# A graph layer's last stage: squares moved behind the next pair's scaling, layer norm in groups of six

## The chip, the cores and the metric

The kernel runs on one core of a Trainium2 chip. The metric is the device time of one execution in microseconds (us); several executions are timed and their median is given. A profile of one execution shows each engine: TensorE (PE, with its weight loads PEld), VectorE (DVE), ScalarE (ACT), GpSimd (POOL) and SyncE (SP), whose queue issues most of the DMAs here.

## The reference

A graph convolution with a mixture of experts, batch norm over the nodes, a residual and a layer norm. There are 6250 nodes of 256 features, 200000 edges and 64 experts, two per node. Cut to what matters:

```python
x = gc + (feats @ W_res + b_res)            # graph convolution and residual weights
core = _moe_ff(x, Wg, bg, w1, b1, w2, b2)   # per node: g1 * expert_1(x) + g2 * expert_2(x)
y = x + core
mean = jnp.mean(y, axis=0)                  # batch norm over the 6250 nodes
var = jnp.mean((y - mean) ** 2, axis=0)
bn = (y - mean) * rsqrt(var + 1e-5) * gamma + beta
z = feats + bn
out = (z - z.mean(-1)) / sqrt(z.var(-1) + 1e-5)   # layer norm over the 256 features
```

## The kernel before

Most of the program (degrees, gathering of neighbours, routing, the 64 experts) is the same before and after. What follows the experts is one block, from line 1552 on, and its instructions keep the order in which the code writes them, engine by engine.

The nodes stand as 50 tiles of 125 nodes (`NT = 50`, `TP = 125`) by 256 features (`D`). `x_all` (or `x`) holds x of all tiles in SBUF, `fb` the features plus beta, also of all tiles. The experts have written their outputs to `y_dram`, two rows per node.

**The gates' stage** takes the tiles in 25 pairs. For each pair it loads `yr` (both experts' rows, 512 KB, eight buffers in the pool `gat`). ACT multiplies the second expert's rows by their gate (line 1576, one instruction for each tile), DVE multiplies the first's by theirs and adds them to x (1578), and DVE adds the second's (1580). ACT squares the pair into `sq` (1582, four buffers of two tiles). TensorE multiplies x and `sq` by a matrix of ones and accumulates the sums over all nodes in `pm` (1584) and `pv` (1586). Two f32 matmuls of 256 columns go to each for every pair.

Then DVE and ACT make `mean`, `scale` (gamma over the standard deviation) and `less` (mean times scale), each 125 x 256 with the same values in all rows (1588 to 1598).

**The layer norm** goes over groups of tiles: 1, 2, 3, then eight groups of five, then 3 and 1. For each group, `scaled` multiplies x by scale on DVE (1622). `sums` adds the features, less offset, to a tile and takes the sum of each node over its features (`accum_out`, 1631); one small instruction turns the sums into minus means `lm` (1633). `squares` on ACT squares with the bias `lm` and sums (1640), one root per group (1642). `rows_out`, one group later, makes the reciprocal `ssq` (1647) and the product of `lm` with it (1648), writes the normalised rows to `o` (DVE 1652 for two tiles of five, ACT 1654 for the rest), and sends them out in two DMAs (112 and 13 partitions).

The features less offset come in two ways. For groups of five, TensorE forms them in PSUM (`pf`, two buffers, 1617): `fb` has a spare partition 125, in which one DMA puts the row `less` for 40 tiles (1610), and the matrix `unit` is an identity with a last row of -1, so that one matmul gives fb - less. `shifted` issues the five matmuls of a group two groups ahead. For the smaller groups DVE subtracts `less` from `fb` in place (1625).

Of the kernel before, what the change touches and what calls it, by code (L numbers as in the profile page):

```python
# [9 lines left out]
F32 = mybir.dt.float32  # L10
# [5 lines left out]
AF = mybir.ActivationFunctionType  # L16
ALU = mybir.AluOpType
# [14 lines left out]
D = 256  # L32
# [117 lines left out]
def gnn_moe_kernel(ctx, tc, x_in, x_cols, src, dst, bases, nexts, firsts, parts, lasts, W_gc, b_gc, W_res, b_res, Wg, bg, w1, b1, w2, b2,  # L150
                   gamma, beta, out):
    nc = tc.nc
    V, S, G, T = nc.vector, nc.scalar, nc.gpsimd, nc.tensor
# [66 lines left out]
    for a in range(0, NS * WMAX, 128):  # L220
        b = min(a + 128, NS * WMAX)
        V.tensor_scalar(iota_h[:, a:b, :], iota_f[:, :b - a, None].to_broadcast([128, b - a, 2]), float(a), None,
                        op0=ALU.add)
# [16 lines left out]
    with tc.tile_pool(name="edges", bufs=1) as ep, ExitStack() as later:  # L240
# [18 lines left out]
        for c, (g0, k, w, n) in enumerate(DENSE):  # L259
            a = g0  # L260
            while a < g0 + k * n:
                b = min(a - a % 2 + LANES // w // 2 * 2, g0 + k * n)
# [3 lines left out]
                a = b  # L266
# [20 lines left out]
        with tc.tile_pool(name="late", bufs=1) as lp, tc.tile_pool(name="both", bufs=2) as bp, \  # L287
# [24 lines left out]
            part = dp.tile([128, 2, ND], F32, name="part")  # L312
# [12 lines left out]
            for k, w in enumerate((W_gc, W_res)):  # L325
                nc.sync.dma_start(out=wcat[:, :, k * D:(k + 1) * D],
                                  in_=w.rearrange("(k p) d -> p k d", p=128))
# [4 lines left out]
            a, wides = 0, []  # L332
            for c, (g0, k, w, n) in enumerate(DENSE):
                if c == ND - 1 or DENSE[c + 1][2] != w:
# [3 lines left out]
                    a = c + 1  # L338
# [11 lines left out]
            for k, values in enumerate((LOW, HIGH)):  # L350
                c = 0
                while c < NC:
                    m = 1
# [139 lines left out]
            for i in range(NGR // CG):  # L493
# [32 lines left out]
                for c in range(CG):  # L526
# [66 lines left out]
        with tc.tile_pool(name="xs", bufs=1) as xs, tc.tile_pool(name="hotg", bufs=2) as hg, \  # L593
# [73 lines left out]
            groups = [(c, j, i) for c, (g0, k, w, n) in enumerate(DENSE) for j in range(n) for i in range(k)]  # L667
# [94 lines left out]
            made = {"below": 0, "above": NT, "gathered": len(GATHER)}  # L762
# [192 lines left out]
            now, n = 0.0, 0  # L955
# [18 lines left out]
            with tc.For_i(0, n_groups, 1) as gi:  # L974
# [6 lines left out]
                                op1=ALU.mult)  # L981
# [3 lines left out]
                                       op0=ALU.mult, op1=ALU.add)  # L985
# [18 lines left out]
                start = ge.tile([128, 1], F32, name="start")  # L1004
# [39 lines left out]
    x = x_all[:TP]  # L1044
# [59 lines left out]
    with tc.tile_pool(name="xw", bufs=1) as xw, tc.tile_pool(name="xl", bufs=3) as xl, \  # L1104
# [42 lines left out]
        with tc.manual_schedule():  # L1147
            sums = {}
            for t0 in range(ta, tb, 2):
                n = min(2, tb - t0)  # L1150
# [8 lines left out]
            for t0, z in sums.items():  # L1159
                n = min(2, tb - t0)  # L1160
# [392 lines left out]
    with tc.tile_pool(name="fin", bufs=1) as fp, tc.tile_pool(name="gat", bufs=8) as gp, \  # L1553
            tc.tile_pool(name="fl", bufs=2) as fl, \
            tc.tile_pool(name="ps_f", bufs=2, space=PSUM) as ps_f, \
            tc.tile_pool(name="ps_m", bufs=1, space=PSUM) as ps_m, tc.manual_schedule():
        unit = fp.tile([128, TP], F32, name="unit")
        below = fp.tile([128, 1], F32, name="below")
        V.tensor_scalar(below, pidx, float(TP), -1.0, op0=ALU.is_ge, op1=ALU.mult)
        V.tensor_scalar(unit, ident[:, :TP], below, None, op0=ALU.add)  # L1560
        eps = fp.tile([TP, 2], F32, name="eps")
        V.memset(eps, LN_EPS)

        S.activation(eps[:, 1:2], eps[:, 0:1], AF.Sqrt)
        pm = ps_m.tile([TP, D], F32, name="pm")
        pv = ps_m.tile([TP, D], F32, name="pv")
        for t0 in range(0, NT, 2):
            yr = gp.tile([128, 2, 2, D], F32, name="yr")
            for t in range(t0, t0 + 2) if t0 < 4 else (t0,):
                n = 1 if t0 < 4 else 2  # L1570
                loads.clear()
                node_in(yr[:, t - t0:t - t0 + n].rearrange("p t j d -> p t (j d)"), y_rows, t, n)
                for u in written[-AHEAD:-1] if t == 0 else ():
                    tc.add_manual_dep(loads[0].ins, u.name, SYNCED, reason="the last writes")
            for t in range(t0, t0 + 2):
                S.activation(yr[:TP, t - t0, 1, :], yr[:TP, t - t0, 1, :], AF.Copy, scale=gates[:, 1, t:t + 1])  # L1576
            for t in range(t0, t0 + 2):
                V.scalar_tensor_tensor(x[:, t, :], yr[:TP, t - t0, 0, :], gates[:, 0, t:t + 1], x[:, t, :],
                                       op0=ALU.mult, op1=ALU.add)
            V.tensor_tensor(x[:, t0:t0 + 2, :], x[:, t0:t0 + 2, :], yr[:TP, :, 1, :], ALU.add)  # L1580
            sq = fl.tile([TP, 2, D], F32, name="sq", bufs=4)
            S.activation(sq, x[:, t0:t0 + 2, :], AF.Square)  # L1582
            for t in range(t0, t0 + 2):
                T.matmul(pm, ones[:TP, :TP], x[:, t, :], start=(t == 0), stop=(t == NT - 1))
            for t in range(t0, t0 + 2):
                T.matmul(pv, ones[:TP, :TP], sq[:, t - t0, :], start=(t == 0), stop=(t == NT - 1))
        mean = fp.tile([TP, D], F32, name="mean")
        V.tensor_scalar(mean, pm, 1.0 / N, None, op0=ALU.mult)
        msq = fp.tile([TP, D], F32, name="msq")
        V.tensor_mul(msq, mean, mean)  # L1590
        scale = fp.tile([TP, D], F32, name="scale")
        V.scalar_tensor_tensor(scale, pv, 1.0 / N, msq, op0=ALU.mult, op1=ALU.subtract)
        V.tensor_scalar(scale, scale, 0.0, BN_EPS, op0=ALU.max, op1=ALU.add)
        S.activation(scale, scale, AF.Sqrt)
        V.reciprocal(scale, scale)  # L1595
        V.tensor_mul(scale, scale, gam)
        less = fp.tile([TP, D], F32, name="less")
        V.tensor_mul(less, mean, scale)


        part = {}
        groups, t0 = [], 0
        for n in [1, 2, 3] + [5] * ((NT - 10) // 5) + [3, 1]:
            groups.append((t0, n))
            t0 += n
        assert t0 == NT

        five = [g for g in groups if g[1] == 5]
        f0, f1 = five[0][0], sum(five[-1])
        nc.sync.dma_start(out=fb[TP:TP + 1, f0:f1, :], in_=less[0:1, None, :].to_broadcast([1, f1 - f0, D]))  # L1610

        def shifted(t0, n):
            if n < 5:
                return
            pf = ps_f.tile([TP, 5, D], F32, name="pf", padded_shape=[TP, 6, D])
            for u in range(5):
                T.matmul(pf[:, u, :], unit[:TP + 1, :], fb[:TP + 1, t0 + u, :], start=True, stop=True)
            part["pf", t0] = pf

        def scaled(t0, n):  # L1620
            xs = x[:, t0:t0 + n, :]
            V.tensor_tensor(xs, xs, scale[:, None, :].to_broadcast([TP, n, D]), ALU.mult)  # L1622
            if n < 5:
                fs = fb[:TP, t0:t0 + n, :]
                V.tensor_tensor(fs, fs, less[:, None, :].to_broadcast([TP, n, D]), ALU.subtract)  # L1625

        def sums(t0, n):
            lm = fl.tile([TP, 5], F32, name="lm", bufs=3)
            for t in range(n):
                f = part["pf", t0][:, t, :] if n == 5 else fb[:TP, t0 + t, :]  # L1630
                V.scalar_tensor_tensor(x[:, t0 + t, :], x[:, t0 + t, :], 1.0, f, op0=ALU.mult,  # L1631
                                       op1=ALU.add, accum_out=lm[:, t:t + 1])
            V.tensor_scalar(lm[:, :n], lm[:, :n], -1.0 / D, None, op0=ALU.mult)  # L1633
            part[t0] = lm

        def squares(t0, n):
            ssq = fl.tile([TP, 5], F32, name="ssq", bufs=3)
            for t in range(n):
                sq = fl.tile([TP, D], F32, name="sq2")
                S.activation(sq, x[:, t0 + t, :], AF.Square, bias=part[t0][:, t:t + 1],  # L1640
                             accum_out=ssq[:, t:t + 1])
            S.activation(ssq[:, :n], ssq[:, :n], AF.Sqrt, scale=1.0 / D, bias=eps[:, 0:1])
            part["ssq", t0] = ssq

        def rows_out(t0, n):
            rs, lm = part.pop(("ssq", t0)), part.pop(t0)
            V.reciprocal(rs[:, :n], rs[:, :n])
            V.tensor_mul(lm[:, :n], lm[:, :n], rs[:, :n])
            o = fl.tile([TP, 5, D], F32, name="o")
            m = 2 if n == 5 else 0  # L1650
            for t in range(m):
                V.tensor_scalar(o[:, t, :], x[:, t0 + t, :], rs[:, t:t + 1], lm[:, t:t + 1], op0=ALU.mult, op1=ALU.add)  # L1652
            for t in range(m, n):
                S.activation(o[:, t, :], x[:, t0 + t, :], AF.Identity, scale=rs[:, t:t + 1], bias=lm[:, t:t + 1])  # L1654
            node_dma(nc.sync, False, o[:, :n, :], node_rows(out, t0, n))

        ahead_of = {i: g for i, g in zip(range(2, len(groups)), five)}
        for i, g in enumerate(groups):
            if i in ahead_of:
                shifted(*ahead_of[i])  # L1660
            scaled(*g)
            sums(*g)
            squares(*g)
            if i:
                rows_out(*groups[i - 1])
        rows_out(*groups[-1])


# [54 lines left out]
```

## Time and profile before

| what | us |
|---|---|
| median of 3 runs | 1546.34 (1545.77 to 1549.16) |
| the profiled execution, its own time | 1543.25 |
| span of its profile | 1541.5 |
| busy: PE 90%, DVE 68%, POOL 51%, ACT 48% of the span | 1380.2, 1047.4, 784.1, 745.3 |
| first load of y issued | 1418.0 after the span's start |
| `less` finished | 1483.5 |
| last ACT instruction ends | 1538.0 |

The span runs from the first to the last instruction; the profiled execution's own time is 1.75 us longer. Times in the views are us from the start of the span. The busy shares are means over stages that have different limits; the part that the change edits is the last 124 us, so its own rows are what to read.

### The profile page before, as it was taken

What the parts mean: (1) busy time and instruction counts of PE and PEld (TensorE: products, weight loads), DVE (VectorE), ACT (ScalarE), POOL (GpSimd) and SP (SyncE); (2) the same over time, 40 slices, a digit from 0 to 9 for tenths busy, and PEclk for the clock granted to TensorE, in tenths of its full rate; (3) what the DMA queues carried; (4) which work ended last, traced back from release to release, by engine and by line L of the source; (5) the groups of instructions that cost most, each with busy time, mean ns of one, the idle gap of its engine ahead of it and who ended that gap; (6) DMA issues with size and microseconds to landing.
All of it is one profiled execution on the core that took longest, in us unless ns stands there. A gap on an engine that the chain in (4) does not pass through costs nothing. (4 is left out here: it accounts for less than half of the span.)

```text
span 1541.5 us, 33071 instructions
## 1 busy us (share of the span) xinstructions
PE 1380.2 (90%) x9987; PEld 1147.4 (74%) x9987; DVE 1047.4 (68%) x2943; ACT 745.3 (48%) x1891; POOL 784.1 (51%) x878
## 2 busy tenths in 40 slices
PE   5999478899999999999999967799999999997963
PEld 3555267788888899999999956688888877875642
DVE  9999889989888888888777749333223233222687
ACT  4675544456666566665555524322222222222668
POOL 7000226777776677766666620376566665652000
PEclk9999699999999999999999978899999999998986
DMA  6899665777777787777777737478687887874804
GB/s 192 263 287 327 241 212 162 209 226 224 210 220 221 204 235 214 217 214 219 218 204 216 203 94 245 130 255 268 203 277 253 277 272 219 250 243 152 286 22 147
DMA packets 209177, 336.41 MB, mean 218 GB/s; under 512 B 22283, under 2 KB 140758, under 8 KB 208989
## 3 DMA queue, kind: packets, MB, share of 16 engines
q1 hardware_dynamic: 154201, 180.36, 37.2%
q0 software_dynamic: 47888, 146.77, 32.4%
q10 hardware_dynamic: 6900, 7.07, 1.6%
q8 instruction: 81, 1.33, 0.4%
q14 instruction: 107, 0.88, 0.2%
HBM read 254.55 MB, written 73.10 MB: 213 GB/s over the span
## 5 line engine op out<-in xcount | busy, mean ns | idle before, releaser
L613 POOL DMA_INDIRECT r<-h_dram,srcg x445 | 468.9, 1054 | 244.1 <-PE pc L699 79.4
L745 PE MATMUL sm<-hrow,counts 128*128 128x258 f32 x1470 | 486.9, 346 | 8.4 <-DVE counts L736 8.3
L719 ACT CAST counts<-pc 128x196 f32 (+7 forms) x879 | 356.9, 406 | 209.0 <-PE pc L699 175.0
L746 PE MATMUL sm<-hrow,counts 128*128 128x256 f32 x1470 | 394.6, 282 | 0.0
L699 PE MATMUL pc<-hotk,lo 128*128 128x245 bf16 (+7 forms) x1118 | 305.0, 304 | 41.7 <-DVE counts L736 19.9
L745 PEld LDWEIGHTS sm<-hrow,counts 128*128 128x128 f32 x1470 | 286.6, 195 | 26.4 <-issue 11.9
L686 DVE TENSOR_TENSOR hotk<-key,iota_h 128x784 bf16<-128x784 f16 (+4 forms) x488 | 246.8, 506 | 58.1 <-PE pc L699 56.0
L746 PEld LDWEIGHTS sm<-hrow,counts 128*128 128x128 f32 x1470 | 279.8, 190 | 1.3
L1442 ACT ACTIVATE hT<-ph,b1c 128x112 f32<-128x112 f32 (+16 forms) x256 | 109.9, 430 | 325.4 <-PE ph L1440 309.9
L736 DVE TENSOR_TENSOR counts<-pc,counts 128x49 f32 x908 | 217.6, 240 | 48.8 <-ACT counts L719 12.3
L1452 PE MATMUL py<-w2s,hT 128*128 128x256 f32 (+7 forms) x992 | 238.0, 383 | 0.0
L1440 PE MATMUL ph<-xgT,w1s 128*128 128x112 f32 (+17 forms) x1024 | 203.0, 342 | 0.6 <-DVE xgT L1430 0.6
L1452 PEld LDWEIGHTS py<-w2s,hT 128*128 128x128 f32 (+7 forms) x992 | 161.0, 170 | 42.2 <-DVE ys L1455 2.5
L1440 PEld LDWEIGHTS ph<-xgT,w1s 128*128 128x128 f32 x1024 | 167.7, 192 | 31.1 <-issue 11.2
L1405 POOL DMA_INDIRECT y_dram<-ys,dest x124 | 119.1, 960 | 112.2 <-DVE ys L1455 63.7
L1455 DVE TENSOR_TENSOR ys<-py,b2s 128x256 f32<-128x256 f32 (+7 forms) x124 | 52.3, 422 | 176.9 <-PE py L1452 167.5
L1405 POOL DMA_INDIRECT xg<-x_dram,ids x124 | 120.3, 970 | 91.9 <-DVE ids L1362 52.9
L699 PEld LDWEIGHTS <-lo 128*128 128x128 bf16 x1118 | 99.5, 100 | 74.7 <-issue 17.4
L618 PE MATMUL pg<-r,hot 128*128 128x258 f32 x445 | 144.6, 325 | 3.1 <-DMA r<-h_dram,srcg 2.3
L1430 DVE TENSOR_SCALAR xgT<-pte,bsum 128x112 f32<-128x112 f32 (+14 forms) x128 | 48.8, 423 | 125.9 <-PE pte L1427 125.8
L619 PE MATMUL pg<-r,hot 128*128 128x256 f32 x445 | 125.1, 281 | 0.0
L457 PE MATMUL pr<-wcat,f 128*128 128x512 f32 x196 | 99.6, 632 | 3.2 <-DMA wcat<-in_L_gnn_W_res_dram 3.2
(330 smaller groups left out, 1724.7 us busy)
## 6 DMA issues: line engine op xcount, KB each, us to landing
w1s<-in_L_gnn_w_dram SPq DMA_DIRECT2D x64, 512.0 KB
w2s<-in_L_gnn_w_dram SPq DMA_DIRECT2D x64, 512.0 KB
y_dram<-zeros SPq DMA_DIRECT2D x48, 256.0 KB
yr<-y_dram SPq DMA_DIRECT2D x22, 512.0 KB
b2s<-in_L_gnn_b_dram SPq DMA_DIRECT2D x64, 128.0 KB
h_dram<-hrow SPq DMA_DIRECT2D x5, 1536.0 KB
r<-h_dram,srcg POOLq DMA_INDIRECT x445
f<-in_x_cols_dram SPq DMA_DIRECT2D x25, 256.0 KB
```

The lines of the kernel that those rows point to most:

```text
L613: G.indirect_dma_start(out=f32(r[:, :2 * D]), out_offset=None, in_=h_dram[:, :], in_offset=bass.IndirectOffsetOnAxis(ap=idx, axis=0))
L618: T.matmul(pg, hot, r[:, D:], start=first, stop=False)
L619: T.matmul(pg[:, :D], hot, r[:, :D], start=False, stop=last)
L686: V.tensor_tensor(hot, pairs(key, e, n, m), iota_h[:, None, :m, :].to_broadcast([128, n // 2, m, 2]), ALU.is_equal)
L699: T.matmul(pc, los[g // PAIRS][:, r // 2, :, r % 2], hots.pop(g), start=(i == 0), stop=(i == k - 1))
L719: put = S.copy(counts[c % 2][:, :, 1:][:, :, ds(at, w - 1)], pc[:, :, 1:])
L736: add = V.tensor_tensor(to, more, f32(had), ALU.add).ins
L745: T.matmul(sm, by, hrow[:, t, D:], start=(t == 0), stop=False)
L746: T.matmul(sm[:, :D], by, hrow[:, t, :D], start=False, stop=(t == NS - 1))
L1405: w = G.indirect_dma_start(**kw)
L1440: T.matmul(ph[:, :m], w1s[:, kk, c * 128:(c + 1) * 128], xgT[:, kk, :m], start=(kk == 0), stop=(kk == 1))
L1452: T.matmul(py[:n], hT[:, c, k * 128:k * 128 + n], w2s[:, c, :], start=(c == 0), stop=(c == 3))
```

## The change

In the gates' stage, the squares and sums of a pair (`summed`) are issued behind the next pair's loading, scaling and adding (`joined`), and `sq` has three buffers instead of four. On ACT, before (`yr_...` and `sq_...` are buffers, one number for each pair):

```order
L1576 ACTIVATE yr_21525<-yr_21525,gates_16387 125x256 x2
L1582 ACTIVATE sq_21532<-x_all_16381 125x512
L1576 ACTIVATE yr_21538<-yr_21538,gates_16387 125x256 x2
L1582 ACTIVATE sq_21545<-x_all_16381 125x512
L1576 ACTIVATE yr_21551<-yr_21551,gates_16387 125x256 x2
```

And from the start of the stage in the changed kernel:

```order
L1584 ACTIVATE yr_21477<-yr_21477,gates_16387 125x256 x2
L1584 ACTIVATE yr_21485<-yr_21485,gates_16387 125x256 x2
L1593 ACTIVATE sq_21493<-x_all_16381 125x512
L1584 ACTIVATE yr_21499<-yr_21499,gates_16387 125x256 x2
L1593 ACTIVATE sq_21506<-x_all_16381 125x512
```

The first square (of the first pair) now stands behind the scaling of the second pair, and so on to the end, where two squares follow each other.

TensorE forms the features less offset for all tiles, two tiles to a matmul (512 columns). The first six tiles are written from `fb` before the gates' stage and left open; when `less` is known, three matmuls of a row of -1 (`minus`, one partition) with `less` close them. The rest comes as before from `fb` with its row of less, now for 44 tiles. On TensorE, the end of the program before, from the last `pv` on:

```order
L1584 MATMUL pm_21469<-x_all_16381,ones_16372 125x256 x2
L1586 MATMUL pv_21470<-sq_21794,ones_16372 125x256 x2
L1617 MATMUL pf_21840<-fb_17227,unit_21462 125x256 x5
L1617 MATMUL pf_21868<-fb_17227,unit_21462 125x256 x5
L1617 MATMUL pf_21902<-fb_17227,unit_21462 125x256 x5
```

The same place in the changed kernel:

```order
L1595 MATMUL pm_21475<-x_all_16381,ones_16372 125x256 x2
L1597 MATMUL pv_21476<-sq_21800,ones_16372 125x256 x2
L1620 MATMUL pf_21471<-less_21816,minus_21469 125x512 x3
L1634 MATMUL pf_21823<-fb_17227,unit_21462 125x512 x3
L1634 MATMUL pf_21870<-fb_17227,unit_21462 125x512 x3
```

The three matmuls with `minus` are new there; `pf_21471` was opened ahead of the first `pm`.

In the layer norm the groups are 1, 2, 3, six groups of six, 4, 3, 1. A group's `scaled` stands one group ahead of its `sums`; the subtraction of less from fb on DVE is gone; `lm` keeps sums, and the factor of minus one over 256 goes into the square's scale and into the product with the reciprocal. Of groups of up to four, the rows go into buffers of the pool `gat` instead of `o`. DVE writes two rows of each group from the fourth on (one of the last, which is one tile). On DVE, behind `less`, before:

```order
L1598 TENSOR_TENSOR less_21810<-mean_21800,scale_21804 125x256
L1622 TENSOR_TENSOR x_all_16381<-x_all_16381,scale_21804 125x256
L1625 TENSOR_TENSOR fb_17227<-fb_17227,less_21810 125x256
L1631 SCALAR_TENSOR_TENSOR x_all_16381,lm_21815<-x_all_16381,fb_17227 125x256
L1633 TENSOR_SCALAR lm_21815<-lm_21815 125x1
L1622 TENSOR_TENSOR x_all_16381<-x_all_16381,scale_21804 125x512
L1625 TENSOR_TENSOR fb_17227<-fb_17227,less_21810 125x512
L1631 SCALAR_TENSOR_TENSOR x_all_16381,lm_21824<-x_all_16381,fb_17227 125x256 x2
L1633 TENSOR_SCALAR lm_21824<-lm_21824 125x2
L1647 RECIPROCAL ssq_21818<-ssq_21818 125x1
L1648 TENSOR_TENSOR lm_21815<-lm_21815,ssq_21818 125x1
```

And in the changed kernel:

```order
L1615 TENSOR_TENSOR less_21816<-mean_21806,scale_21810 125x256
L1638 TENSOR_TENSOR x_all_16381<-x_all_16381,scale_21810 125x256
L1638 TENSOR_TENSOR x_all_16381<-x_all_16381,scale_21810 125x512
L1644 SCALAR_TENSOR_TENSOR x_all_16381,lm_21828<-x_all_16381,pf_21471 125x256
L1638 TENSOR_TENSOR x_all_16381<-x_all_16381,scale_21810 125x768
L1644 SCALAR_TENSOR_TENSOR x_all_16381,lm_21835<-x_all_16381,pf_21471 125x256 x2
L1659 RECIPROCAL ssq_21830<-ssq_21830 125x1
L1660 SCALAR_TENSOR_TENSOR lm_21828<-lm_21828,ssq_21830 125x1
L1638 TENSOR_TENSOR x_all_16381<-x_all_16381,scale_21810 125x1536
L1644 SCALAR_TENSOR_TENSOR x_all_16381,lm_21851<-x_all_16381,pf_21471 125x256 x3
```

Scaling of the next group stands ahead of a group's sums, and the first sum reads `pf` in PSUM where it read `fb`. The diff, cut:

```diff
+SIZES_OUT = [1, 2, 3] + [6] * 6 + [4, 3, 1]
+PIECES = list(range(0, 43, 6)) + [46, N // TP]
...
+        minus = fp.tile([1, TP], F32, name="minus")
+        V.memset(minus, -1.0)
+        pf = [ps_f.tile([TP, 6, D], F32, name="pf")]
+        for t in range(0, 6, 2):
+            T.matmul(pf[0][:, t:t + 2, :], unit[:TP, :], fb[:TP, t:t + 2, :], start=True, stop=False)
...
-            sq = fl.tile([TP, 2, D], F32, name="sq", bufs=4)
+
+        def summed(t0):
+            sq = fl.tile([TP, 2, D], F32, name="sq", bufs=3)
             S.activation(sq, x[:, t0:t0 + 2, :], AF.Square)
...
+        for t0 in range(0, NT, 2):
+            joined(t0)
+            if t0:
+                summed(t0 - 2)
+        summed(NT - 2)
...
+        nc.sync.dma_start(out=fb[TP:TP + 1, 6:, :], in_=less[0:1, None, :].to_broadcast([1, NT - 6, D]))
+        for u in range(0, 6, 2):
+            T.matmul(pf[0][:, u:u + 2, :], minus, less[0:1, None, :].to_broadcast([1, 2, D]), start=False, stop=True)
...
+        def shifted(k):
+            pf.append(ps_f.tile([TP, 6, D], F32, name="pf"))
+            a, b = PIECES[k:k + 2]
+            for t in range(a, b, 2):
+                T.matmul(pf[k][:, t - a:t - a + 2, :], unit[:TP + 1, :], fb[:TP + 1, t:t + 2, :], start=True, stop=True)
...
-            if n < 5:
-                fs = fb[:TP, t0:t0 + n, :]
-                V.tensor_tensor(fs, fs, less[:, None, :].to_broadcast([TP, n, D]), ALU.subtract)
...
-            V.tensor_scalar(lm[:, :n], lm[:, :n], -1.0 / D, None, op0=ALU.mult)
...
-                S.activation(sq, x[:, t0 + t, :], AF.Square, bias=part[t0][:, t:t + 1],
+                S.activation(sq, x[:, t0 + t, :], AF.Square, scale=-float(D), bias=part[t0][:, t:t + 1],
...
-            V.tensor_mul(lm[:, :n], lm[:, :n], rs[:, :n])
-            o = fl.tile([TP, 5, D], F32, name="o")
-            m = 2 if n == 5 else 0
+            V.scalar_tensor_tensor(lm[:, :n], lm[:, :n], -1.0 / D, rs[:, :n], op0=ALU.mult, op1=ALU.mult)
+            if n > 4:
+                o = fl.tile([TP, 6, D], F32, name="o")
+            else:
+                o = gp.tile([128, 2, 2, D], F32, name="yr").rearrange("p t j d -> p (t j) d")[:TP]
+            m = 0 if t0 < 6 else min(n, 2)
...
+        scaled(*groups[0])
+        made = 1
         for i, (t0, n) in enumerate(groups):
+            if made < len(PIECES) - 1 and (i > 2 or made < 2):
+                shifted(made)
+                made += 1
+            if i + 1 < len(groups):
+                scaled(*groups[i + 1])
+            sums(t0, n)
+            squares(t0, n)
             if i:
                 rows_out(*groups[i - 1])
```

More of the change, by code (lines that the diff above doesn't have):

```diff
@@ L1564, in gnn_moe_kernel, with joined @@
         S.activation(eps[:, 1:2], eps[:, 0:1], AF.Sqrt)
+        minus = fp.tile([1, TP], F32, name="minus")
[3 more added lines that the diff above has]
+            T.matmul(pf[0][:, t:t + 2, :], unit[:TP, :], fb[:TP, t:t + 2, :], start=True, stop=False)
         pm = ps_m.tile([TP, D], F32, name="pm")
         pv = ps_m.tile([TP, D], F32, name="pv")
-        for t0 in range(0, NT, 2):
+        def joined(t0):
             yr = gp.tile([128, 2, 2, D], F32, name="yr")
@@ L1598, in gnn_moe_kernel @@
         V.tensor_mul(less, mean, scale)
+        nc.sync.dma_start(out=fb[TP:TP + 1, 6:, :], in_=less[0:1, None, :].to_broadcast([1, NT - 6, D]))
+        for u in range(0, 6, 2):
+            T.matmul(pf[0][:, u:u + 2, :], minus, less[0:1, None, :].to_broadcast([1, 2, D]), start=False, stop=True)
         part = {}
         groups, t0 = [], 0
-        for n in [1, 2, 3] + [5] * ((NT - 10) // 5) + [3, 1]:
+        for n in SIZES_OUT:
             groups.append((t0, n))
@@ L1606, in gnn_moe_kernel @@
         assert t0 == NT
[L1608 to L1612, printed above, removed]
-            if n < 5:
[L1614 to L1618, printed above, removed]
+        def shifted(k):
[3 more added lines that the diff above has]
+                T.matmul(pf[k][:, t - a:t - a + 2, :], unit[:TP + 1, :], fb[:TP + 1, t:t + 2, :], start=True, stop=True)
         def scaled(t0, n):
@@ L1622, in scaled @@
             V.tensor_tensor(xs, xs, scale[:, None, :].to_broadcast([TP, n, D]), ALU.mult)
-            if n < 5:
-                fs = fb[:TP, t0:t0 + n, :]
-                V.tensor_tensor(fs, fs, less[:, None, :].to_broadcast([TP, n, D]), ALU.subtract)
         def sums(t0, n):
[L1628 to L1633, printed above, removed]
+            lm = fl.tile([TP, 6], F32, name="lm", bufs=3)
+            for t in range(t0, t0 + n):
+                k = max(k for k in range(len(PIECES)) if PIECES[k] <= t)
+                V.scalar_tensor_tensor(x[:, t, :], x[:, t, :], 1.0, pf[k][:, t - PIECES[k], :], op0=ALU.mult,
+                                       op1=ALU.add, accum_out=lm[:, t - t0:t - t0 + 1])
             part[t0] = lm
         def squares(t0, n):
-            ssq = fl.tile([TP, 5], F32, name="ssq", bufs=3)
+            ssq = fl.tile([TP, 6], F32, name="ssq", bufs=3)
             for t in range(n):
                 sq = fl.tile([TP, D], F32, name="sq2")
-                S.activation(sq, x[:, t0 + t, :], AF.Square, bias=part[t0][:, t:t + 1],
+                S.activation(sq, x[:, t0 + t, :], AF.Square, scale=-float(D), bias=part[t0][:, t:t + 1],
                              accum_out=ssq[:, t:t + 1])
-            S.activation(ssq[:, :n], ssq[:, :n], AF.Sqrt, scale=1.0 / D, bias=eps[:, 0:1])
+            S.activation(ssq[:, :n], ssq[:, :n], AF.Sqrt, scale=1.0 / D ** 3, bias=eps[:, 0:1])
             part["ssq", t0] = ssq
@@ L1655, in rows_out @@
             node_dma(nc.sync, False, o[:, :n, :], node_rows(out, t0, n))
[L1657 to L1663, printed above, removed]
+        scaled(*groups[0])
+        made = 1
+        for i, (t0, n) in enumerate(groups):
+            if made < len(PIECES) - 1 and (i > 2 or made < 2):
[5 more added lines that the diff above has]
+            squares(t0, n)
             if i:
```

## The prediction

> **What bounds the kernel now.** The change touches only the end of the program, so I read the page first for the size of that end, then the chain of work that ended last, then the timeline of the end by engine, then stretches of time with the granted clock.
>
> ```profile
> span 1541.5 us, 33071 instructions
> ```
>
> The part that the change edits is the last 124 us of this span. It has two stages: the gates' products with the batch statistics (1418 to 1483.5), and the layer norm (1483.5 to the end).
>
> In the first stage the chain (start, duration, what) repeats this for each pair of tiles:
>
> ```profile
> 1470.77 0.63 ACT sq L1582
> 1471.40 0.81 ACT yr L1576 x2
> 1472.23 0.70 DVE x_all L1580
> 1472.97 0.04 issue
> 1473.01 0.63 ACT sq L1582
> ```
>
> A pair takes 1473.01 - 1470.77 = 2.24 us. No engine is full: the time is a ring. ACT squares pair k, then scales pair k+1, then DVE adds pair k+1, and only then can ACT square pair k+1. The same pair by the timeline of ACT and DVE, with what each engine waited for:
>
> ```profile
> 1469.98 0.69 DVE L1580 TENSOR_TENSOR x_all<-x_all,yr 125x512 f32<-125x512 f32 x1 [0.76 <-ACT yr L1576]
> 1470.59 0.88 DVE L1578 SCALAR_TENSOR_TENSOR x_all<-yr,gates,x_all 125x256 f32<-125x256 f32 x2
> 1470.77 0.63 ACT L1582 ACTIVATE sq<-x_all 125x512 f32<-125x512 f32 x1 [0.82 <-DVE x_all L1580]
> 1471.30 0.89 ACT L1576 ACTIVATE yr<-yr,gates 125x256 f32<-125x256 f32 x2
> ```
>
> By themselves DVE needs at most 0.69 + 0.88 = 1.57 us for a pair and ACT 0.63 + 0.89 = 1.52; the rest is waiting for each other. TensorE's own rate shows where it had a backlog:
>
> ```profile
> 1428.04 1.03 PE L1586 MATMUL pv<-sq,ones 125*125 125x256 f32 x4
> ...
> 1433.22 1.03 PE L1586 MATMUL pv<-sq,ones 125*125 125x256 f32 x4
> ```
>
> Six groups of two matmuls in 5.18 us, 0.863 a group, so a pair (two groups) costs TensorE 1.73 us. The stretches (length, PE, PEld, DVE, ACT, POOL busy, granted clock, DMA share, GB/s):
>
> ```profile
> 1100.00:1140.00 40.00, 40.00 (x215) 34.80 (x215) 12.55 (x32) 10.71 (x25) 27.09 (x26) 1.00 0.87 275
> 1430.00:1434.00 4.00, 4.00 (x20) 3.29 (x18) 2.53 (x7) 2.86 (x6) 0.00 (x0) 1.00 1.05 393
> 1450.00:1454.00 4.00, 3.52 (x15) 2.79 (x16) 2.48 (x7) 2.86 (x6) 0.00 (x0) 1.00 0.73 230
> 1478.00:1482.00 4.00, 1.46 (x7) 0.94 (x5) 2.71 (x5) 0.55 (x2) 0.00 (x0) 1.00 0.00 0
> 1482.00:1484.00 2.00, 0.00 (x0) 0.00 (x0) 1.93 (x5) 0.00 (x0) 0.00 (x0) 0.54 0.00 0
> ```
>
> A TensorE that is busy throughout keeps clock 1.00 (first two rows). The loads of y reach 393 GB/s when buffers are free; at 512 KB a pair that is 1.33 us, so they are not the pace either.
>
> **The gates' stage.** ACT's order becomes: scale pair k+1, then square pair k. The square's input was added while ACT scaled, so the ring is gone, and a pair takes the largest of 1.57 (DVE), 1.52 (ACT), 1.33 (loads) and 1.73 (TensorE): TensorE. The start and the end:
>
> ```profile
> 1418.57 0.29 DVE L1560 TENSOR_SCALAR unit<-ident,below 128x125 f32<-128x125 f32 x1
> 1423.22 2.07 PE L1584 MATMUL pm<-x_all,ones 125*125 125x256 f32 x4 [9.45 <-DMA yr<-y_dram]
> 1424.36 0.48 DVE L1578 SCALAR_TENSOR_TENSOR x_all<-yr,gates,x_all 125x256 f32<-125x256 f32 x1 [0.61 <-DMA yr<-y_dram]
> 1478.43 1.03 PE L1586 MATMUL pv<-sq,ones 125*125 125x256 f32 x4
> 1483.11 0.43 DVE L1598 TENSOR_TENSOR less<-mean,scale 125x256 f32<-125x256 f32 x1
> ```
>
> The opening three matmuls of pf (six tiles) start at about 1418.9, when unit is there. At half clock two tiles took 2.07 us (second row; start to start 0.86 a tile), so they take 5.2 and end at about 1424.0, 0.8 after the first pm could start. That is hidden: the first square now stands behind the scaling of pair 1, whose load comes at 1424.36 (third row), so it ends at 1424.36 + 0.45 (half of the 0.89) + 0.63 = 1425.5, and TensorE waits for that. If they were dearer, each us would be one of the end. Then pv of pair 0, pm and pv of pair 1 take 3 x 0.863, to 1428.1, and the other 23 pairs 39.7: TensorE ends at 1467.9 instead of 1479.46, **-11.5**; I take -11.4 for a wait or two. Everything up to less shifts with it. The bounds: DVE's 1.57 a pair would give -15; a handover of 0.3 us left in each pair gives 2.03 a pair and -5.4. The ring of squares drops from four tiles to three: a square waits for the pv three pairs back, while TensorE has two pairs (3.5 us) in its queue, and behind the square on ACT stands only the next 0.89 of scaling, so I cost it at nothing. The -1 row costs one memset beside the loads. SP's queue keeps its order (loads of y, the row of less, outputs), and POOL has nothing here.
>
> **The layer norm, its start.** In the times of before:
>
> ```profile
> 1484.24 0.42 DVE L1631 SCALAR_TENSOR_TENSOR x_all<-x_all,fb 125x256 f32<-125x256 f32 x1
> 1487.02 9.47 PE L1617 MATMUL pf<-fb,unit 126*125 126x256 f32 x30 [7.56 <-DMA fb<-less]
> 1483.87 0.34 DVE fb L1625
> 1485.46 0.61 DVE fb L1625
> 1488.20 0.88 DVE fb L1625
> ```
>
> Removed: the three subtractions on DVE (last rows), 1.83 us. New: the first sum waits for three matmuls minus x less of two tiles each, and TensorE signals only behind the third, so the sum waits for all. They can start when less ends, 4.1 us after TensorE's last pv, and the clock had by then fallen (1.00 until 1482, 0.54 after). Their price is not in the trace: six tiles at 0.43 each are 2.6 at full clock, 5.2 at half. The row at 1487.02 has fifteen tiles in 9.47 us, where full clock would give 6.5 and half clock 12.9: it was slow for its first 5 to 6 us. So the clock returns at best near the end of the three; I take 4.6 and keep 2.6 to 5.2. The first sum then runs at 1483.5 + 4.6 + 0.2 = 1488.3 instead of 1484.24: four us lost, behind which DVE has only the 0.95 of two scalings to do. From there DVE does, in its new order, a sum 0.45, scaling three tiles 0.87, two sums 0.8, reciprocal and product 0.4, scaling six 1.75 (1.41 for five, on the chain below, plus 0.27, the step between the last rows here, and its drain), three sums 1.1, 0.4 again, six scaled 1.75 and small gaps 0.2: the sums of the first six begin at 1496.0. ACT's square of a tile now waits for that tile's sum alone, since the means' own multiply is gone: it starts at 1496.5. The second pf is written behind the -1 products from 1488.3, 2.6 to 5.2 us long, hidden by DVE until 1496.0; the row for it (44 tiles instead of 40) landed at 1487.02, also before.
>
> **The layer norm, its pace.** One group of five, on the chain and on ACT where it did not wait:
>
> ```profile
> 1502.46 0.17 DVE lm L1633
> ...
> 1502.96 0.73 DVE o L1652 x2
> 1503.70 1.41 DVE x_all L1622
> 1505.23 1.81 DVE x_all L1631 x10
> 1507.06 0.18 DVE lm L1633
> ```
>
> ```profile
> 1498.54 0.49 ACT L1640 ACTIVATE sq<-x_all,lm 125x256 f32<-125x256 f32 x1
> 1501.12 0.30 ACT L1642 ACTIVATE ssq<-ssq,eps 125x5 f32<-125x5 f32 x1
> 1501.33 1.57 ACT L1654 ACTIVATE o<-x_all,lm,ssq 125x256 f32<-125x256 f32 x3
> 1502.80 0.49 ACT L1640 ACTIVATE sq<-x_all,lm 125x256 f32<-125x256 f32 x1
> ```
>
> Before, DVE sets 4.60 for five (0.92 a tile), ACT needs 4.26. After, for six: DVE 4.60 + one more scaling 0.27 + one more sum 0.36 - the multiply 0.17 = 5.1; ACT 5 x 0.49 + 0.62 (squares) + 0.21 (root) + 4 x 0.49 (rows, two still on DVE) = 5.24, or 0.87 a tile: ACT becomes the pace. From 1496.5 ACT has 44 squares (35 x 0.49 + 9 x 0.62), nine roots (1.9) and 30 rows (14.7), 39.3 in all, to 1535.8.
>
> ```profile
> 1537.41 0.60 ACT L1654 ACTIVATE o<-x_all,lm,ssq 125x256 f32<-125x256 f32 x1 [1.76 <-DMA out_dram<-o]
> ```
>
> ```profile
> 1533.32 0.32 SPq L180
> ```
>
> Before, ACT ended at 1538.01 after waiting 1.76 us for an output buffer; groups of up to four now take the free y buffers, and the last row goes to DVE. So ACT ends 2.2 earlier. Of that I give back 0.7: the last two groups' four output DMAs are then issued close together (before: the last group's two), each 0.32 by the chain's row of the queue, and behind 768 KB and 512 KB still moving. The layer norm: **-1.5**.
>
> **Sum.** -11.4 - 1.5 = -12.9: span 1528.6, and 1530.3 for the execution whose own time was 1543.25. That execution stands 3.1 below the median of the three runs, 1546.34; on that median the forecast is **1533.4 us**. A measurement of this kernel tells about 0.2% (3.1 us) from no change.
>
> **The rivals.** First, the clock stays full across the 4.1 us gap: the three products take 2.6, the first sum comes 2 earlier, 1531.4. Against it stands the fall to 0.54 at about 1482.2, 2.7 us after the last pv. The Trainium skill (TensorE: Matmul & The Clock Gate, What's actually happening) has the throttle return after at least one idle window of about 3.4 us that runs freely; by that rule alone a gap of 4.1 would hold a whole idle window in only some executions, and this rival would be the usual case. The trace does not agree with so strict a rule: 2.7 us of idleness were enough here.
>
> Second, a handover stays in each pair of the gates' stage (ACT's square tied to TensorE by three tiles): 2.03 a pair, 1546.34 - 5.4 - 1.5 = 1539.4. For it: TensorE idle 0.48 of 4 us in the row at 1450, a little in each pair; against: two pairs in its queue.
>
> Third, the loads pace the stage: in the row at 1450 they moved only 230 GB/s, which is 2.28 us a pair and no gain, 1544.8. Against: that was the pace of buffer release, and 393 stands in the row of 1430.
>
> Fourth, slower: TensorE, busy throughout, is granted less than 0.77 of its clock in the gates' stage (1.73 / 2.24). At 0.5 a pair costs 3.46, 25 x 1.22 = 30 us more, 1575. Against: 1.00 in the rows at 1100 and 1430.
>
> **How the numbers follow.** The forecast 0.64 (its own range 1531 to 1536, from 2.6 to 5.2 for the products and one us of tail), full clock 0.14, handover 0.13, loads 0.05, slower 0.04. Faster 0.91, same 0.05, slower 0.04. The range 1529.5 to 1539.5 reaches from the full clock less the scatter of runs to the handover.
>
> **What would show it.** Right: pm and pv groups every 0.86 us without a wait from about 1428, clock 1.00; less about 11.4 earlier; DVE's first sum waiting some 4 us for the minus matmuls; ACT without waits in the groups of six, 5.2 apart; no wait for out_dram at the end. Wrong: ACT's squares waiting for pv with TensorE idle, a clock under 1.00 there, DVE waiting for output buffers (768 KB now), or ACT starved between groups.

## The result, and the profile after

The changed kernel takes **1534.17 us** (median of six executions, 1533.89 to 1535.65) and the kernel before 1546.76 in the same comparison: 0.9919 of the time, 95% interval 0.9906 to 0.9932, faster by 12.6 us (10.5 to 14.5). The forecast was 1533.4, the range 1529.5 to 1539.5. The profiled execution took 1535.01 us.

```profile
span 1533.3 us, 33022 instructions
```

The gates' stage first. The chain of work that ended last (start, duration, what) was a ring of ACT and DVE before. Now it is TensorE alone:

```profile
1441.26 0.86 PE pv L1597 x4
1442.12 0.86 PE pm L1595 x4
1442.98 0.86 PE pv L1597 x4
1443.85 0.86 PE pm L1595 x4
```

Two groups are a pair: 1442.98 - 1441.26 = 1.72 us, against 2.24 before. The stretches (length, PE, PEld, DVE, ACT, POOL busy, granted clock, DMA share, GB/s) show TensorE without a gap and at clock 1.00, with and without loads beside it:

```profile
1440.00:1444.00 4.00, 4.00 (x20) 3.48 (x19) 3.79 (x9) 3.52 (x8) 0.00 (x0) 1.00 1.06 388
1460.00:1464.00 4.00, 4.00 (x21) 3.45 (x20) 3.69 (x8) 3.49 (x9) 0.00 (x0) 1.00 0.01 4
```

The stage's ends, from the timeline: the first load of y, the opening matmuls, the one late load, and the last group.

```profile
1420.33 3.02 SPq L190 DMA_DIRECT2D yr<-y_dram  x5
1421.52 4.91 PE L1571 MATMUL pf<-fb,unit 125*125 125x512 f32 x6 [5.51 <-DVE minus L1568]
1426.27 1.03 PE L1595 MATMUL pm<-x_all,ones 125*125 125x256 f32 x4
1429.15 0.91 ACT L1584 ACTIVATE yr<-yr,gates 125x256 f32<-125x256 f32 x2 [1.78 <-DMA yr<-y_dram]
1430.63 1.13 PE L1597 MATMUL pv<-sq,ones 125*125 125x256 f32 x4 [1.22 <-ACT sq L1593]
1470.45 1.03 PE L1597 MATMUL pv<-sq,ones 125*125 125x256 f32 x4
```

From the first load's issue to the end of the last pv: 1471.48 - 1420.33 = 51.15 us. Before it was 1479.46 - 1417.98 = 61.48.

Then the layer norm's start. DVE and ACT wait for the -1 products, and the clock, which fell behind the last pv, stays at half through all of them and well into the second pf:

```profile
1475.60 5.48 PE L1620 MATMUL pf<-less,minus 1*125 1x512 f32 x6 [4.13 <-DVE less L1615]
1481.12 0.42 DVE L1644 SCALAR_TENSOR_TENSOR x_all<-x_all,pf 125x256 f32<-125x256 f32 x1 [4.63 <-PE pf L1620]
1487.91 0.42 DVE L1644 SCALAR_TENSOR_TENSOR x_all<-x_all,pf 125x256 f32<-125x256 f32 x1
1488.37 0.51 ACT L1652 ACTIVATE sq<-x_all,lm 125x256 f32<-125x256 f32 x1
```

```profile
1472.00:1474.00 2.00, 0.00 (x0) 0.00 (x0) 1.49 (x3) 0.42 (x1) 0.00 (x0) 0.88 0.00 0
1476.00:1480.00 4.00, 4.00 (x5) 1.39 (x5) 0.48 (x1) 0.00 (x0) 0.00 (x0) 0.50 0.18 11
1484.00:1486.00 2.00, 2.00 (x3) 0.39 (x2) 2.00 (x8) 1.29 (x5) 0.00 (x0) 0.50 0.18 50
1486.00:1488.00 2.00, 2.00 (x4) 0.87 (x4) 1.97 (x6) 1.97 (x8) 0.00 (x0) 0.71 0.05 14
1488.00:1490.00 2.00, 1.49 (x4) 0.37 (x2) 2.00 (x13) 1.93 (x8) 0.00 (x0) 1.00 0.38 105
```

The pace and the end, on ACT's and DVE's timelines (in order: two squares, an output on DVE, the last rows of ACT and of DVE):

```profile
1498.40 0.49 ACT L1652 ACTIVATE sq<-x_all,lm 125x256 f32<-125x256 f32 x1
1503.65 0.49 ACT L1652 ACTIVATE sq<-x_all,lm 125x256 f32<-125x256 f32 x1
1518.83 0.74 DVE L1667 TENSOR_SCALAR o<-x_all,ssq,lm 125x256 f32<-125x256 f32 x2 [0.88 <-DMA out_dram<-o]
1527.26 0.58 ACT L1669 ACTIVATE yr<-x_all,lm,ssq 125x256 f32<-125x256 f32 x1
1527.78 0.41 DVE L1667 TENSOR_SCALAR yr<-x_all,ssq,lm 125x256 f32<-125x256 f32 x1
```

The first two rows are the first squares of two neighbouring sixes: 5.25 us a six on ACT, with no wait between. DVE did wait for an output buffer in the last two sixes, 0.53 and 0.88 us (third row), but ACT never waited between its square at 1488.37 and its last row. The last row of the output is made at 1528.19. The span ends 5.11 us later; before, that was 1541.5 - 1538.01 = 3.49. In between, the outputs still move at some 260 GB/s:

```profile
1527.00:1529.00 2.00, 0.00 (x0) 0.00 (x0) 0.73 (x3) 0.81 (x3) 0.00 (x0) 0.50 0.90 265
1529.00:1531.00 2.00, 0.00 (x0) 0.00 (x0) 0.00 (x0) 0.00 (x0) 0.00 (x0) 0.50 0.89 257
```

**All stages in one table**, for every kernel that follows. Each column is worked out as above, from the issue of the first load of y, the start of the first pm, the end of the last pv and the end of the span, in us. What lies ahead of the first load is unchanged and scatters (1417.8 to 1423.5 over the ten profiles of the first, third and fourth sets), so these lengths tell more than whole times do. The span is printed to 0.1 us, so the last column of lengths is good to 0.05.

| kernel | first load to first pm | to last pv | to end | median; ratio to before, interval |
|---|---|---|---|---|
| before | 5.24 | 56.24 | 62.04 | 1546.76 |
| before, again | 6.32 | 56.16 | 62.05 | 1.0004, 0.9987-1.0020 |
| after | 5.94 | 45.21 | 61.82 | 1534.17; 0.9919, 0.9906-0.9932 |
| after, again | 6.35 | 45.00 | 61.82 | 0.9915, 0.9895-0.9934 |
| gates' order alone | 5.70 | 46.10 | 62.07 | 0.9939, 0.9921-0.9958 |
| gates' order undone | 5.91 | 55.23 | 61.74 | 0.9987, 0.9974-1.0000 |
| few pv products | 6.16 | 40.53 | 61.74 | 1533.44; 0.9917, 0.9895-0.9939 |
| gap filled | 5.91 | 44.91 | 60.05 | 1532.66; 0.9909, 0.9893-0.9925 |
| -1 products over 125 rows | 6.39 | 44.68 | 60.74 | 1533.89; 0.9917, 0.9899-0.9935 |
| outputs of sixes halved | 5.48 | 44.42 | 61.12 | 1533.88; 0.9920, 0.9905-0.9934 |
| gap filled, 125 rows | 6.52 | 43.99 | 59.14 | 1533.45; 0.9911, 0.9892-0.9929 |
| outputs halved, four too | 6.13 | 44.79 | 60.91 | 1534.05; 0.9920, 0.9904-0.9936 |
| five rows to DVE | 6.02 | 45.20 | 60.10 | 1532.78; 0.9903, 0.9888-0.9919 |
| all four edits | 6.29 | 43.99 | 56.66 | 1529.43; 0.9882, 0.9865-0.9900 |

The second set (the rows "again" and the gates' order) ran in a session in which every kernel took some 54 us longer ahead of the first load, so it is told in ratios and lengths. In the third set (few pv products to outputs of sixes halved) the kernel before took 1546.68, in the fourth 1547.44. Two executions far above all others (4706 us in after, again and 5001 us in few pv products) are left out of the medians here.

### The profile page after: what moved, and what is told of

It is laid out like the page before. It is cut to its first block, busy times and chain, and to the rows that moved or that the text cites. A ratio compares the mean times of both kernels' runs of the same rounds, so it can differ in the third digit from the quotient of the medians.

```text
span 1533.3 us, 33022 instructions
## 1 busy us (share of the span) xinstructions
PE 1382.8 (90%) x9963; PEld 1141.8 (74%) x9963; DVE 1045.5 (68%) x2924; ACT 743.7 (49%) x1889; POOL 779.0 (51%) x878
## 3 DMA queue, kind: packets, MB, share of 16 engines
q8 instruction: 81, 1.33, 0.4%
## 5 line engine op out<-in xcount | busy, mean ns | idle before, releaser
L1442 PEld LDWEIGHTS ph<-xgT,w1s 128*128 128x128 f32 x1024 | 167.6, 191 | 31.3 <-issue 11.2
```

The lines of the kernel that those rows point to most:

```text
L1442: T.matmul(ph[:, :m], w1s[:, kk, c * 128:(c + 1) * 128], xgT[:, kk, :m], start=(kk == 0), stop=(kk == 1))
```

## The experiments

**Both kernels again.** Unchanged.

> The kernel before, once more, for a second profile. Two things could explain that the edited end is 10.6 us shorter in the two profiles (from the first load of y to the end of the span, 123.5 against 113.0 us) while the medians differ by 12.6. Theory A: the end is the same in every execution and the part ahead of it scatters by some us; then this profile has 123.5 +- 0.4 for the end whatever its own time. Theory B: the first profile of before had a lucky end; then this end is about 125.5.

> The changed kernel, once more. Theory A: the end is 113.0 +- 0.4 us again, whatever the execution's own time. Theory B: the first profile had an unlucky end (the second load of y was late by about 1 us); then it is 111 to 112 us, and TensorE's last pv ends 50 us after the first load of y instead of 51.15.

Measured: ends of 124.53 and 113.17 us. The second is what theory A said. The first lies between the two theories: 1.0 more than in the first profile, and 1.08 of it ahead of the first pm, where the first loads landed later. From the last pv on, both kernels repeat to within 0.05 us. So the stages' lengths are the kernels' own, up to the arrival of the first loads, and the two pairs of profiles give (61.98 - 51.25) + (62.05 - 61.82) = 11.0 us for the change. That lies inside the interval of the times (10.5 to 14.5). The 1.6 us up to the medians' difference were not found in any edited stage.

**Gates' order alone.** To the kernel before:

```
-        for t0 in range(0, NT, 2):
+        def joined(t0):
...
-            sq = fl.tile([TP, 2, D], F32, name="sq", bufs=4)
+        def summed(t0):
+            sq = fl.tile([TP, 2, D], F32, name="sq", bufs=4)
...
+        for t0 in range(0, NT, 2):
+            joined(t0)
+            if t0:
+                summed(t0 - 2)
+        summed(NT - 2)
```

> The kernel before with the gates' stage alone changed: scaling and adding of pair k+1 are written ahead of the squares and products of pair k; the layer norm stays in fives, and the opening three matmuls stand where they stood. Theory (the gates' stage carries the change): TensorE's groups 0.863 us apart, 10.3 us less than before, the time 1536 to 1537 us, within 2.5 us of the whole change. Rival (the layer norm in sixes carries a good part, 3 us or more): 1539 or above.

Measured: 46.10 from the first pm, 10.1 less than before, and 0.9939 of the time against 0.9915 for the whole change. By the medians of this set the two are 2.9 us apart (1590.81 and 1587.95), a little more than the 2.5 expected; by their lengths from the first pm to the end, 1.1 to 1.4. The order of the gates' stage carries the change. Its TensorE starts cold (granted clock 0.50), where the changed kernel's is at 1.00 from 1425.7 on, ahead of its first pm; the timeline of TensorE and a stretch:

```profile
1478.23 2.07 PE L1588 MATMUL pm<-x_all,ones 125*125 125x256 f32 x4 [10.16 <-DMA yr<-y_dram]
1480.10 1.91 PE L1590 MATMUL pv<-sq,ones 125*125 125x256 f32 x4
1481.80 1.91 PE L1588 MATMUL pm<-x_all,ones 125*125 125x256 f32 x4
```

```profile
1480.00:1482.00 2.00, 2.00 (x6) 1.52 (x6) 0.78 (x2) 0.78 (x2) 0.00 (x0) 0.50 0.99 359
```

Three groups take about 1.8 us each, where 0.86 is the price at full clock. Here the squares kept their four buffers. With three, in the changed kernel, ACT waits for pv at the last squares (1.8 us in four waits), while TensorE has work throughout, so the stage is no slower.

**Gates' order undone.** To the changed kernel:

```
             joined(t0)
-            if t0:
-                summed(t0 - 2)
-        summed(NT - 2)
+            summed(t0)
```

> The changed kernel with the squares and products of each pair written directly behind its own sums again; opening matmuls, -1 products and groups of six stay. Theory: a pair costs 2.24 us again by the ring of ACT and DVE, and the layer norm gives 0.2 us in the profile (1.5 in the prediction's sum): 1545 to 1546.5 us. Rival (the new layer norm is worth 3 us or more by itself): 1543.5 or below.

The ring is back, in the chain of waits:

```profile
1501.70 0.81 ACT yr L1584 x2
1502.51 0.02 issue
1502.53 0.70 DVE x_all L1588
...
1503.32 0.63 ACT sq L1593
1503.95 0.81 ACT yr L1584 x2
```

1503.95 - 1501.70 = 2.25 us a pair. Against before the stage is 1.0 shorter from the first pm (55.23 against 56.20), and the layer norm 0.3. Most of that 1.0 is no gain: the opening matmuls are still running when DVE has added the first pair (L1588), and the first pm starts 0.76 behind that instead of 0.05. From the end of that addition to the last pv it is 55.99, against 56.29 and 56.22 in the two profiles of before. The whole time, 0.9987 of before (0.9974 to 1.0000), shows no clear gain. The warm start shows where TensorE is the bound: gates' order alone, at half clock to begin with, has its last pv 5.65 behind the last square, the changed kernel 4.51, and its stage is 1.0 longer (46.10 against 45.1).

**Few pv products.** To the changed kernel:

```
-            for t in range(t0, t0 + 2):
+            for t in range(t0, t0 + 2) if t0 in (0, NT - 2) else ():
                 T.matmul(pv, ...)
```

> The changed kernel without 23 of the 25 pairs of pv's products (the first and the last pair keep theirs): the variance is left incomplete, everything else is done. Theory (TensorE's 1.73 us a pair sets the stage): the pace falls to the next limit, DVE's own 1.57 us a pair, so TensorE's end comes 23 x 0.16 = 3.7 us earlier and the span 3 to 4 us. Rival 1 (ACT and DVE still wait for each other, and TensorE only follows): no gain, within 0.5 us. Rival 2 (the loads of y set it at 1.33 us a pair and DVE's work overlaps): 9 us less.

Measured: 40.53, or 4.6 less. TensorE now waits for DVE in each pair, and DVE does not wait (the timelines, and a stretch):

```profile
1442.15 1.13 PE L1595 MATMUL pm<-x_all,ones 125*125 125x256 f32 x4 [0.46 <-DVE x_all L1588]
1443.74 1.13 PE L1595 MATMUL pm<-x_all,ones 125*125 125x256 f32 x4 [0.46 <-DVE x_all L1588]
```

```profile
1440.00:1444.00 4.00, 2.62 (x10) 1.60 (x10) 3.79 (x9) 3.52 (x8) 0.00 (x0) 1.00 1.05 383
```

1.59 us a pair, DVE's price and not the loads' 1.33. So TensorE was the bound of the changed stage, and DVE stands only 0.14 a pair behind it: the next step there would be worth some 3 us and no more. Of the 4.6, 3.1 are TensorE's backlog (the last pv ends 1.38 behind the last square instead of 4.51); the rest lies ahead of the last square: the first loads landed closer together in this profile (the second square starts 2.3 behind the first, against 3.2 and 2.8 in the two profiles of the changed kernel), and ACT no longer waits for pv at the end.

**The gap filled.** Four matmuls of two tiles behind the last pv; pf[1], in which they write, is allocated there:

```
+        pf.append(ps_f.tile([TP, 6, D], F32, name="pf"))
+        for u in range(4):
+            T.matmul(pf[1][:, 0:2, :], unit[:TP, :], fb[:TP, 0:2, :], start=True, stop=True)
         mean = fp.tile([TP, D], F32, name="mean")
```

> The changed kernel with four more matmuls of two tiles between the last pv and the -1 products (about 3.5 of the 4.07 us in which TensorE waits for less); their results are overwritten. Theory A (the -1 products are dear because TensorE was idle ahead of them): clock 1.00 through them, 2.6 us instead of 5.5, the first sum 2.9 us earlier, and ACT's first square of the first six as much earlier; the end 1.5 to 2.9 earlier. Theory B (products with one row of weights do not count as work for the clock): they begin at 1.00, but the clock falls within the next 3.4 us or so, the second pf runs at half clock; the first sum is still 2.5 to 2.9 earlier. Rival (DVE's two scalings and the sums that follow hide it, or the last outputs are bound by their transfers): less than 0.7 us at the end.

```profile
1469.48 3.60 PE L1606 MATMUL pf<-fb,unit 125*125 125x512 f32 x8
1473.78 3.79 PE L1623 MATMUL pf<-less,minus 1*125 1x512 f32 x6 [0.70 <-DVE less L1618]
```

```profile
1473.00:1475.00 2.00, 1.30 (x4) 0.65 (x4) 1.63 (x4) 0.00 (x0) 0.00 (x0) 1.00 0.00 0
1475.00:1477.00 2.00, 2.00 (x4) 0.51 (x2) 0.00 (x0) 0.00 (x0) 0.00 (x0) 0.63 0.35 23
1477.00:1479.00 2.00, 2.00 (x3) 0.82 (x3) 1.40 (x4) 0.90 (x3) 0.00 (x0) 0.50 0.00 0
```

The products start at full clock and take 3.79 instead of 5.48, because the clock falls under them, at about 1475.5, while TensorE is busy. That is theory B, though its 2.5 to 2.9 us were too much: the fall comes early under the products, and 1.7 are saved. All of these are found at the end of the span (60.05 against 61.82), so the rival, that the end hides it, falls.

**The -1 products over 125 rows.**

```
-        minus = fp.tile([1, TP], F32, name="minus")
-        V.memset(minus, -1.0)
+        minus = fp.tile([TP, TP], F32, name="minus")
+        V.memset(minus, 0.0)
+        V.memset(minus[0:1], -1.0)
...
-            T.matmul(pf[0][...], minus, less[0:1, None, :].to_broadcast([1, 2, D]), ...)
+            T.matmul(pf[0][...], minus, less[:, None, :].to_broadcast([TP, 2, D]), ...)
```

> The changed kernel with the -1 products made over 125 rows (a matrix whose first row is -1 and whose others are 0, against all rows of less): the same sums, the same columns, the same number of matmuls. Theory B (the one-row products kept TensorE busy for 5.5 us but were not counted as work): the clock is back 3.4 to 6.8 us after the first of them starts, instead of 11.6, and the second pf runs at full clock (2.6 us instead of 5.2). Theory A (they count, and the clock came back late for another reason, the phase of its windows): 10 us or more again. The time of the kernel by either: within 1 us of the changed kernel, since DVE hides the second pf.

```profile
1475.69 4.41 PE L1621 MATMUL pf<-less,minus 125*125 125x512 f32 x6 [4.13 <-DVE less L1616]
1479.94 2.74 PE L1635 MATMUL pf<-fb,unit 126*125 126x512 f32 x6
```

```profile
1475.00:1477.00 2.00, 1.31 (x2) 0.79 (x3) 1.54 (x4) 0.00 (x0) 0.00 (x0) 0.62 0.00 0
1477.00:1479.00 2.00, 2.00 (x3) 0.69 (x3) 0.00 (x0) 0.00 (x0) 0.00 (x0) 0.53 0.35 23
1479.00:1481.00 2.00, 2.00 (x6) 0.94 (x5) 0.86 (x3) 0.40 (x1) 0.00 (x0) 1.00 0.00 0
```

The clock is back at about 1478.9, 3.2 us after these products start (a little less than the 3.4 expected), and not 11.6. The second pf takes 2.74. The end comes 1.08 us earlier, since the last of the products already run at full clock, which neither theory had counted.

**Outputs of sixes halved.** The output of a six is sent as tiles 0 to 2 and 3 to 5. This version does not send the last tile's output at all (128 KB).

```
+            h = 3 if n == 6 else n
...
-            node_dma(nc.sync, False, o[:, :n, :], node_rows(out, t0, n))
+                if t + 1 in (h, n):
+                    a = 0 if t + 1 == h else h
+                    node_dma(nc.sync, False, o[:, a:t + 1, :], node_rows(out, t0 + a, t + 1 - a))
```

> The changed kernel with the output of each group of six sent in two halves (three tiles when ACT has done the first of its four rows, three behind the last). Theory (the last 1.8 MB are issued together and move at some 270 GB/s, so the span ends 5.1 us after the last row): the time from the last row to the end of the span falls from 5.1 to about 3.5, the kernel 1 to 1.6 us faster. Rival (the 3.5 us are the fixed cost of the last transfers, or the issues on the queue at 0.3 us each are what is late): no change, or up to 0.6 slower by the twelve more issues.

Measured: 61.12, 0.7 less, but with one transfer fewer, so it decides nothing, and was made anew below.

**Both edits on the -1 products.**

> The changed kernel with both edits at once: four filling matmuls in TensorE's wait for less, and the -1 products over 125 rows. Theory (TensorE's clock falls for idleness, and one-row products count as idleness; the first sum's wait is a term of the end one to one): the clock stays 1.00 through the products, they take 2.6 to 2.7 us instead of 5.5, the first sum comes 2.9 us earlier and so does the end, from the last pv 58.9 us instead of 61.8. Rival (the clock falls for the 0.7 us of idleness that are left): 3.8 us or more for the products, the end 1.7 us earlier as with the filling alone.

```profile
1475.19 2.84 PE L1624 MATMUL pf<-less,minus 125*125 125x512 f32 x6 [0.70 <-DVE less L1619]
1478.83 2.84 PE L1639 MATMUL pf<-fb,unit 126*125 126x512 f32 x6 [0.80 <-DMA fb<-less]
```

```profile
1473.00:1475.00 2.00, 1.49 (x4) 0.37 (x2) 1.93 (x3) 0.00 (x0) 0.00 (x0) 1.00 0.00 0
1477.00:1479.00 2.00, 1.20 (x4) 0.36 (x3) 0.94 (x3) 0.47 (x2) 0.00 (x0) 1.00 0.27 17
```

As the theory has it: clock 1.00 throughout, 2.84 instead of 5.48 (2.6 to 2.7 were expected), and 59.14 to the end, 2.7 less. The second pf now waits 0.80 for the row of less to land, a wait that the slow products had hidden. The whole time shows 1.2 of these 2.7 by the ratios (0.9911 against 0.9919), but its interval is 5.7 us wide.

**Outputs halved, the four's too.** As above, with every tile sent; the group of four goes in halves as well.

> The changed kernel with the outputs of each group of six and of the group of four sent in two halves, every tile sent. Theory (about 1 MB in the last three groups' outputs, issued within 3.5 us, is bound by some 270 GB/s): from the last row to the end 4.6 us or less instead of 5.1, the end up to 0.7 earlier. Rival (the extra issues on the queue, 0.3 us each or more, and the fixed cost of the last transfer hold the end): 5.1 or more.

Measured: 60.91, 0.9 less, and 4.22 from the last row to the end. The theory's size holds (4.6 or less, and 0.7), its reason only in part: the queue's rows for the last groups (count, shortest, median and longest issue in ns) show that in the changed kernel the issues themselves are slow and late. First after, then before:

```profile
L182 SPq DMA_DIRECT2D out_dram<-yr x6: 318/468/707, 1526.6 to 1529.9; - x6
```

```profile
L180 SPq DMA_DIRECT2D out_dram<-o x8: 317/360/475, 1530.0 to 1538.4; - x8
```

The last issue starts 1529.9 - 1528.19 = 1.7 us behind the last row, and some 0.4 before (1538.4 against 1538.01), while the transfers of the two groups ahead still move. That it is these transfers that slow the issues was not tried apart.

**Five rows to DVE.** In rows_out, with rows up to m on DVE:

```
-            m = 0 if t0 < 6 else min(n, 2)
+            m = 0 if t0 < 6 else 2 if t0 < 24 else min(n, 3)
```

> The changed kernel with one more row a group on DVE instead of ACT in the last three sixes, the group of four and the group of three (five rows, 0.49 each on ACT). Theory (ACT is the pace of the layer norm, and DVE runs some us ahead of it at the end): ACT ends 2.4 us earlier, the last row 2 to 2.4 earlier; the end 1 to 2.4 earlier, the less the more the last outputs are bound by their transfers. Rival (DVE is as full as ACT, so its later reciprocals and sums hold ACT up): less than 0.5 us.

Measured: the last row 1.9 earlier behind less (50.74 against 52.65), the end 1.7 earlier. ACT was the pace, and DVE had room for most of it: ACT's own last row comes 3.3 earlier (49.01 against 52.30), and DVE's last row, the one that counts, now ends 1.73 behind it instead of 0.35.

**All four edits.**

> All of it: filling matmuls, -1 products over 125 rows, five rows moved to DVE, outputs of sixes and of the four in halves. If the gains add: 2.9 + 2.2 + 0.5 = 5 to 5.6 us less than the changed kernel, about 1529 us where the changed kernel takes 1534. If the last outputs' transfers become the bound: 3 to 4 us less.

Measured: 56.66 from the last pv, 5.2 less than the changed kernel; the single gains, 2.7 + 0.9 + 1.7 = 5.3, add. The time is 1529.43, 0.9882 of before (0.9865 to 0.9900), which does not touch the changed kernel's interval in the first comparison (0.9906 to 0.9932), but does overlap that of its repeat (0.9895 to 0.9934). It beats the kernel before clearly; that it beats the changed kernel rests on the lengths (5.2 us) more than on the times.

## Why the prediction was right, and where a size was off

- **The gates' stage, -11.4.** Right in mechanism and nearly in size: TensorE at 1.72 a pair, clock 1.00, less earlier. By the two profiles of each kernel it is -10.7; with the seven other kernels whose stage is the same (51.2 to 49.9 from the first load) -11.2. In the first profile one load came late (1.78 on ACT, 1.22 on TensorE). Few pv products shows that TensorE is the bound, and DVE's price, costed at 1.57 and measured at 1.59, the next. The three buffers of squares made ACT wait at the end, but cost TensorE nothing, as forecast.
- **The opening matmuls, costed at nothing.** In the new order they are worth about 1.0, since TensorE starts at full clock; in the old order next to nothing. The sum held this tacitly: it counted the first groups at 0.863 each, which holds only behind such work.
- **The handover (1539.4), the loads (1544.8), the lower clock (1575).** None shows: TensorE has no gap from the late load's pv at 1430.63 to the last, the stage runs at 388 GB/s while loads last, and the clock is 1.00.
- **The -1 products, 4.6 with 2.6 to 5.2.** 5.48: outside the range, since the clock did not return within them. The first sum started 5.57 behind less instead of 4.8, yet the first six's sums began 12.4 behind less, where 12.5 was forecast: DVE's work in between was 0.9 shorter than its terms. That the two errors cancel is luck.
- **The full clock across the gap (1531.4).** It did not come by itself. Filling the gap did not give this rival's 2.6 us either: the clock fell under the one-row products, which took 3.79. With products over 125 rows as well, the clock holds and saves 2.7 at the end, where the forecast had 2.0: the products it replaces took 5.48 and not 4.6.
- **ACT as the pace, 5.24 a six and 39.3 in all.** 5.25, and 1527.84 - 1488.37 = 39.5. ACT ends 2.2 earlier behind less (54.47 to 52.29), as forecast. DVE's waits for output buffers, which the prediction listed as a sign of being wrong, came (0.53 and 0.88) without holding ACT.
- **Given back at the end, 0.7.** This is the failed term. From ACT's end to the span's end it is 5.46 instead of 3.49, so 2.0 is given back. The issues were costed at 0.32 each, and took 0.32 to 0.71; DVE's last row also ends 0.35 behind ACT's. So the layer norm gives 0.2, not 1.5.
- **The sum.** The stages give about -11.0 to -11.4 and the times -12.6; the forecast's -12.9 agrees with the times, in part because the layer norm's 1.3 too much is no larger than the scatter. So the gates' stage was understood; that the whole came within 0.3 us of the measured difference is in part luck.

## What to carry to other kernels

Where the chain shows two engines in turn on one pair of tiles, writing the second engine's next piece ahead of its answer takes out the ring, and the pace is then the largest of the engines' own prices, which can be read from rows without waits. The gates' gain reached the end whole, but a gain in the last rows is worth its size only as far as the outputs can follow (ACT ended 2.2 earlier, the span 0.2): count the issues and the bytes behind the last row, and send large outputs in parts. Where a few matmuls stand behind a gap on the path, keep the clock by filling the gap, and give the filling and the few matmuls themselves many rows (125 here).

## What the runs showed of the hardware, unexpected

The clock did not follow TensorE's busy time alone. Products with one row of weights, back to back for 5.5 us, did not bring it back: in the changed kernel's profile it returned 11.6 us after the first, when 126-row matmuls had run for 6. In the six other profiles with these products behind an unfilled gap it returned 8.3 to 9.6 us after the first, and in none while they ran. With the gap filled it fell under one-row products. The same products over 125 rows brought it back in 3.2 us, and with the gap filled they held it, in both profiles that have them. Between 1 and 125 rows nothing was tried.

In each profile the changes of the granted clock lie whole multiples of 3.41 us apart (1425.72, 1473.51 and 1487.16 in the changed kernel's: 14 and 4 times). That helps with the rival that the 0.70 us of idleness brought the fall in the filled gap. In the 3.41 us before that fall (1472.12 to 1475.53) TensorE was busy for 80% with the one-row products counted, and for 28% without them. In the stage of few pv products, 65% (2.62 of 4.00) kept clock 1.00. So the fall fits only if the one-row products do not count in full.

The Trainium skill (TensorE: Matmul & The Clock Gate, What's actually happening) has the clock gated by how busy TensorE has been, with release after a busy window of about 3.4 us. The 3.2 us over 125 rows come near that, a little short of a whole window; the one-row products, busy throughout by the trace, do not agree with it. And where the gap was not filled, the fall came 2.0 to 4.5 us after the last pv, in several profiles sooner than the whole idle window of which that section speaks.
